# Moving weight preparation ahead of the image in a windowed-attention and convolution block

## The chip, the cores and the metric

The kernel runs on one core of one Trainium2 chip. A core has five engines that run side by side: TensorE (PE, matrix products), VectorE (DVE), ScalarE (ACT), GpSimd (POOL) and SyncE (SP), which here only issues transfers. Sixteen DMA engines move data between main memory (HBM) and the on-chip memory SBUF; matrix products land in a second on-chip memory, PSUM. Engines wait for each other and for transfers through semaphores. The metric is the device time of one launch in microseconds (us), as the median of several runs.

## The reference, cut to what matters

The input x is float32, 8 images of 384 channels and 64 x 64 pixels. Two layers follow each other:

```
x = x + attention(group_norm(x))          # layer 0
x = x + filtered_conv(group_norm(x))      # layer 1
```

`group_norm` takes 32 groups of 12 channels per image, and subtracts the mean and divides by the standard deviation over all pixels of a group. Layer 0 normalises each pixel over its 384 channels (`(xt - mu) / sqrt(var + eps) * norm_g + norm_b`), forms queries, keys and values by one product with `qkv_w`, and attends within 8 x 8 windows: half of the channels in plain windows, the other half in windows shifted by 4 pixels with a mask, four heads of 48 each with a table of position biases. A product with `proj_w` follows. Layer 1 is a product with `w_in`, a filter on the 8 x 8 Fourier transform of each block, a 3 x 3 convolution by channel, a gated gelu and a product with `w_out`.

## The kernel before, in words

**Tiling.** An image is cut into 8 strips of 8 rows (512 pixels, 8 windows). A strip in SBUF is 128 partitions by 3 chunks by 512 pixels, 0.79 MB. All products are in float32. A trace shows two matmul records for each matmul of the code.

**Schedule.** Every piece of work is a Python function, and a list `plan` holds pieces with a place on a time line (`at(place, piece, ...)`, L721 to L805). One unit of it is one window stage of attention; image b starts at 16 b. The list is sorted and the pieces are issued in that order (L811 to L827). Matmuls keep exactly this order on TensorE (`tc.keep_in_program_order` in `matmul`, L62). The other engines' instructions are placed by a scheduler unless they are held to the order in the same way. Ahead of the loop of L811, a count of TensorE instructions is kept for each piece (`FETCHES`, four for a matmul, two for a transpose); where `small_tiles` stands in the plan, up to 99 empty instructions are spread over neighbouring large matmuls so that the following dense run begins at a chosen position modulo 256 (`RUN_AT`).

**The prologue of the first image.** All loads of the start are issued at the top of the kernel. SP's queue takes the eight strips of the first image (`first_x`, L92), then the constants `cst` (identity, averaging matrices, masks; L95), the query and key weights in two raw tiles (`wqk_raw`, L113), the value weights `wv`, then `wp`, `w_in` (L119) and `w_out`. ScalarE's queue takes small vectors (`vec`, L141 and L143: gains and biases, most of them 4 bytes a row). GpSimd's queue takes the two tables of position biases in 64 transfers (`rpb_raw`, L171). A transfer increments one of eight semaphores that SP's and ScalarE's queues share, and it waits until the earlier transfer on its semaphore has landed.

Then, in the order of the plan: `input_stats` (L237) for the eight strips, `input_mean` and `input_std` (two tiny products, `pm_a` and `pv_a`), `group_normal` of the first strips (L328, gives y), and the sums for the normalisation over channels. That is three pieces. `ln_square` squares y on ScalarE (L333) and adds the three chunks on GpSimd (L335). `ln_sums` forms means of y (12 matmuls) and of the squares (4) with a matrix of ones, copies them, and computes the reciprocal standard deviation `rc` of 4 rows of 128 pixels. Those are written to DRAM as one line and read back to all 128 partitions (`rs`, L356 and L358). `ln_scale` multiplies y by `rs` (L363). The gain and the mean of that normalisation are worked into the weights instead: `pack_qk` copies the raw weights into 6 blocks per chunk (26 copies, L135), `qk_weights` (for each of the two branches) and `v_weights` form the bias from `lnb` (`pb`, `pv`), and `centre` scales by `lng` (L198), forms the column mean by three matmuls (`pc`) and subtracts it (L202).

In the plan, these stand at -3.02 (`pack_qk`), -2.9 (`qk_weights` of branch 0), -0.95 (`v_weights`) and -0.94 (`qk_weights` of branch 1), between the sums of the first strips.

**Attention.** The dense work begins with `qk_tile` (`pq`, L391), three tiles of three matmuls for a strip and a branch, evicted by ScalarE (L394), then `v_tile` (`pvv`), `scores` (`pS`), softmax, `turn` (`pT`), `apply` (`pA`), `put` and `project`. The second branch reads a shifted copy of two neighbouring strips, which GpSimd makes from the scaled y (L376 to L378).

Of the kernel before, what the change touches and what calls it, by code (L numbers as in the profile page):

```python
# [9 lines left out]
ALU = mybir.AluOpType  # L10
AX = mybir.AxisListType

P = 128
KC = 3
C = 384
# [3 lines left out]
NS = SW // WS  # L19
# [11 lines left out]
FETCHES = {"qk_tile": 12, "v_tile": 24, "project": 12, "scores": 128, "apply": 128, "turn": 16, "put": 16,  # L31
           "ln_sums": 64, "mix": 12, "transform": 32, "back": 192, "finish": 48, "input_mean": 4,
           "input_std": 4, "second_mean": 4, "second_std": 4, "filter_weights": 4, "out_bias": 36,
           "qk_weights": 48, "v_weights": 60}
RUN_AT = 208, 138


# [1 line left out]
def block_kernel(ctx: ExitStack, tc: tile.TileContext, out, x, consts, fsel, wqk, wv, bqk, bv,  # L39
                 wp, bp, lng, lnb, rpb1, rpb2, w_in, w_dw, w_out, filt):  # L40
    nc = tc.nc
# [8 lines left out]
    def psum(name):  # L50
        return ps.tile([P, ST], F32, tag="gemm", name=name)
# [9 lines left out]
    def matmul(*args, **kw):  # L61
        tc.keep_in_program_order(nc.tensor.matmul(*args, **kw))  # L62
        fetched["count"] += 4

        n = min(fetched["empty"], fetched["share"])
        for _ in range(n):
            tc.keep_in_program_order(nc.tensor.nop(hint="empty"))
        fetched["empty"] -= n
        fetched["count"] += n
# [5 lines left out]
    def strip(tag, bufs, name):  # L75
        return sb.tile([P, KC, ST], F32, tag=tag, bufs=bufs, name=name)
# [4 lines left out]

    def rows_of(img, s):

        return img[:, s * WS:(s + 1) * WS, :].rearrange("(p k) h w -> p k (h w)", k=KC)

    first_x = []
    for s in range(NS):
        tag, bufs = ("x", 5) if s < 5 else (("xn", 1), ("ow", 1), ("y2", 1))[s - 5]  # L90
        t = strip(tag, bufs, f"x_first{s}")
        nc.sync.dma_start(out=t, in_=rows_of(x[0], s))  # L92
        first_x.append(t)
    cst = cp.tile([P, N_CONST], F32, name="cst")
    nc.sync.dma_start(out=cst, in_=consts)  # L95
    ident = cst[:, C_ID:C_ID + P]
# [18 lines left out]
    wv_sb = cp.tile([P, KC, C], F32, name="wv_sb")  # L115
    wp_sb = cp.tile([P, KC, C], F32, name="wp_sb")
    wi_sb = cp.tile([P, KC, C], F32, name="wi_sb")
    for dst, src in ((wv_sb, wv), (wp_sb, wp), (wi_sb, w_in)):
        nc.sync.dma_start(out=dst, in_=src)  # L119
    wo_sb = cp.tile([P, 2, C], F32, name="wo_sb")  # L120
    nc.sync.dma_start(out=wo_sb[:, 0, :], in_=w_out[0:P])
# [6 lines left out]
        blocks += [(1, 96, 16, 1, 1, 32), (1, 112, 16, 1, 1, 96)] if j == 1 else [(j, 96, 32, 1, 1, c)]  # L128
    by_branch = wqk_sb.rearrange("p k (b j) c -> p k b j c", b=2)

    def pack_qk():
        for br in range(2):
            for i, (j, to, n, t, hp, of) in enumerate(blocks):
                eng = nc.gpsimd if br and i % 2 else nc.vector
                eng.tensor_copy(by_branch[:, :, br, j, to:to + n], raw_qk[t][:, :, br, hp, of:of + n])  # L135

    vec = cp.tile([P, 18], F32, name="vec")
    lng_sb, lnb_sb = vec[:, 0:3], vec[:, 3:6]
# [54 lines left out]

    bq_sb = cp.tile([P, 2, 6], F32, name="bq_sb")

    def centre(w):
        for k in range(KC):
            nc.vector.tensor_scalar(w[:, k], w[:, k], lng_sb[:, k:k + 1], None, ALU.mult)  # L198
        pc = psum("pc")
        for k in range(KC):  # L200
            matmul(pc[:, 0:C], ones_c, w[:, k], start=(k == 0), stop=(k == KC - 1))
        nc.vector.tensor_tensor(w, w, pc[:, 0:C].unsqueeze(1).to_broadcast([P, KC, C]), ALU.subtract)  # L202

    def qk_weights(br):
        pb = psum("pb")
        for j in range(3):
            for k in range(KC):
                matmul(pb[:, j:j + 1], wqk_sb[:, k, 3 * br + j, :], lnb_sb[:, k:k + 1],
                       start=(k == 0), stop=(k == KC - 1))
        own = bqk_sb[:, 3 * br:3 * br + 3]  # L210
        tc.keep_in_program_order(nc.vector.tensor_tensor(own, own, pb[:, 0:3], ALU.add))

        for i in range(2):
            nc.vector.tensor_scalar(bq_sb[:, i, 3 * br:3 * br + 3], own, pick[:, i:i + 1], None, ALU.mult)
        centre(wqk_sb[:, :, 3 * br:3 * br + 3].rearrange("p k j c -> p k (j c)"))

    def v_weights():
        pv = psum("pv")
        for lo, hi, kt, cols in ((0, P, 0, 0), (0, 64, 1, 192), (64, P, 1, 128), (0, P, 2, 256)):
            for k in range(KC):  # L220
                matmul(pv[lo:hi, kt:kt + 1], wv_sb[:, k, cols:cols + hi - lo], lnb_sb[:, k:k + 1],
                       start=(k == 0), stop=(k == KC - 1))
        nc.vector.tensor_tensor(bv_sb, bv_sb, pv[:, 0:3], ALU.add)
        centre(wv_sb)

    def out_bias():
        pp = psum("pp")
# [49 lines left out]
    def at(place, piece, *args):  # L277
        plan.append((place, len(plan), piece, args))
# [44 lines left out]
    def group_normal(b, s):  # L323
# [3 lines left out]
        for k in range(KC):  # L327
            nc.vector.tensor_scalar(by_window(y[:, k, :]), image_order(t[:, k, :]), gs[:, 0:1], gs[:, 1:2],  # L328
                                    ALU.subtract, ALU.mult)

    def ln_square(b, s):
        sq = ys[b, s, "sq"] = strip("sq", 1, f"sq_{b}_{s}")
        nc.scalar.activation(sq, ys[b, s], AF.Square)  # L333
        for k in (1, 2):
            nc.gpsimd.tensor_tensor(sq[:, 0, :], sq[:, 0, :], sq[:, k, :], ALU.add)  # L335

    def ln_sums(b, s):


        p = psum(f"ln_{b}_{s}")  # L340
        for to, t, n in ((0, ys[b, s], KC), (P, ys.pop((b, s, "sq")), 1)):
            for k in range(n):
                for j in range(4):
                    matmul(p[32 * j:32 * (j + 1), to:to + P], ones_c[:, 0:32], t[:, k, j * P:(j + 1) * P],
                           start=(k == 0), stop=(k == n - 1))
        m = sb.tile([P, 2 * P], F32, tag="lc", bufs=1, name=f"m_{b}_{s}")
        nc.scalar.copy(m, p[:, 0:2 * P])  # L347
        rc = sb.tile([P, P], F32, tag="lr", bufs=2, name=f"lr_{b}_{s}")
        nc.vector.tensor_tensor(rc, m[:, 0:P], m[:, 0:P], ALU.mult)  # L349
        nc.vector.tensor_tensor(rc, m[:, P:2 * P], rc, ALU.subtract)  # L350
        nc.scalar.activation(rc, rc, AF.Sqrt, bias=eps_t)
        nc.vector.reciprocal(rc, rc)

        line = dr.tile([4, P], F32, tag="line", bufs=4, name=f"line_{b}_{s}")
        queue = nc.scalar if b == 0 and s < 2 else nc.sync
        queue.dma_start(out=line, in_=rc[0:P:32, :])  # L356
        rs = ys[b, s, "rs"] = row512("rs", 2, f"rs_{b}_{s}")
        queue.dma_start(out=rs, in_=bass.AP(line.tensor, line.offset, [[0, P], [1, ST]]))  # L358

    def ln_scale(b, s):  # L360

# [359 lines left out]
    for b in range(B):  # L721
# [4 lines left out]
            at(u, load, b, s, "stats")  # L726
            at(u + (0.5 if b else 0.05), input_stats, b, s)
        if b == 0:
            at(-3.02, pack_qk)
            at(-2.9, qk_weights, 0)  # L730
            at(-0.95, v_weights)
            at(-0.94, qk_weights, 1)
            at(-0.9, position_bias, 0)
            at(-0.5, position_bias, 1)
            at(0.2, out_bias)
            at(0.2, filter_weights)
# [76 lines left out]
    for i, (piece, args) in enumerate(order):  # L813
        count += 4 * sum(on_pe[args[1]].values()) if piece is conv_taps else FETCHES.get(piece.__name__, 0)
        if piece in (qk_tile, project):
            dense.append(i)
        elif piece is scores:
            dense = []
        elif piece is small_tiles:
            n = (RUN_AT[args[0] % 2] - count - round(WAITS[0] * args[0] + WAITS[1])) % 256  # L820
            if n < 100:
                count += n
                for j in range(n):
                    empty[dense[j % len(dense)]] += 1
# [111 lines left out]
```

## Time and profile before

| | us |
|---|---|
| median of 3 runs | 3713.88 |
| lowest, highest | 3712.17, 3715.45 |
| the profiled execution's own time | 3717.37 |
| its span, from first to last instruction | 3715.4 |
| mean granted TensorE clock, share of full | 0.995 |

A line of the timeline gives the start in us from the first instruction, the duration, the engine, the line of the kernel, the operation, the tile written and the tiles read, shapes, and how many instructions were merged (x8). In brackets stands the idle time of that engine before it and who ended it; "issue" means that the profile shows no one. PEld is the loading of weights into TensorE. A row of the list of waits has the waiting engine and tile, the one waited for, the total in us, the number of waits and the longest. PEclk is the share of the full TensorE clock that was granted in a stretch.

### The profile page before, as it was taken

The numbers are of one execution on the slowest core, as the hardware profiler recorded it, in microseconds if no ns is written. First come the engines' busy times: TensorE is split into PE (matmuls) and PEld (weight loads), VectorE is DVE, ScalarE is ACT, GpSimd is POOL, SyncE is SP. The second block draws the span as 40 slices with busy tenths as digits, with TensorE's granted clock in tenths as the row PEclk, the third lists the DMA queues.
The fourth block names the chain that finished last, engine by engine and source line by source line (L and its number), as shares of the span: only waits on it lengthen the run. The fifth ranks groups of instructions, "written<-read, shape, count | busy, mean of one in ns | idle before, by whom it ended". The sixth has DMA issues, their size and how long they took to land.

```text
span 3715.4 us, 92922 instructions
## 1 busy us (share of the span) xinstructions
PE 3609.1 (97%) x38528; PEld 2340.4 (63%) x38528; DVE 2844.0 (77%) x4601; ACT 2383.0 (64%) x3946; POOL 435.1 (12%) x776
## 2 busy tenths in 40 slices
PE   4999999999999999999999999999999999999898
PEld 2666666666666666666666666666666666666554
DVE  4555568777887788787887778877788777777898
ACT  1766676666676576675776667676676766676442
POOL 5111111011111011101111011111011111110000
PEclk9999999999999999999999999999999999999999
DMA  4222222233232233222332332323232322222422
GB/s 122 80 89 75 92 100 102 87 111 109 101 123 84 89 134 109 104 94 104 107 130 84 109 106 101 132 82 105 88 131 102 107 89 84 100 81 81 154 103 77
DMA packets 144507, 377.34 MB, mean 102 GB/s; under 512 B 12308, under 2 KB 12900, under 8 KB 144100
## 3 DMA queue, kind: packets, MB, share of 16 engines
q1 hardware_dynamic: 139952, 370.60, 28.4%
q8 instruction: 319, 5.23, 0.6%
q0 software_dynamic: 2048, 0.15, 0.1%
q10 hardware_dynamic: 2100, 0.63, 0.1%
q14 instruction: 88, 0.72, 0.1%
HBM read 270.54 MB, written 100.79 MB: 100 GB/s over the span
## 4 chain that ended last, share of the span: by engine, by line
PE 86%; DVE 6%; DMA 4%; ACT 2%; issue 1%; POOL 0%; SPq 0%; DVEq 0%; ACTq 0%; POOLq 0%
PE pq L62 24%; PE pr L62 13%; PE pvv L62 12%; PE pt L62 12%; PE pw L62 6%; DVE zz L673 3%; PE pS L62 3%; PE pA L62 3%; PE pT L72 3%; PE po L72 3%; PE pz L62 3%; PE pf L62 2%; PE ln L62 2%; DMA x_norm<-in_x_dram 1%; DMA rpb_raw<-in_rpb_dram 1%
## 5 line engine op out<-in xcount | busy, mean ns | idle before, releaser
L673 DVE SCALAR_TENSOR_TENSOR zz<-z,dw_sb,zz 128x512 f32<-128x512 f32 x1490 | 1081.8, 751 | 23.7 <-ACT z L632 11.2
L62 PE MATMUL pq<-y,wqk_sb 128*128 128x512 f32 x2160 | 990.2, 596 | 0.0
L62 PEld LDWEIGHTS pq<-y,wqk_sb 128*128 128x128 f32 x2160 | 402.7, 190 | 437.1 <-issue 403.9
L62 PE MATMUL pt<-wi_sb,xn 128*128 128x384 f32 x1536 | 534.6, 486 | 0.0
L62 PE MATMUL pr<-oT,wp_sb 128*128 128x512 f32 x1152 | 523.1, 592 | 0.4 <-DVE oT L537 0.4
L62 PE MATMUL pvv<-wv_sb,y 128*128 128x192 f32 x2880 | 495.8, 326 | 0.0
L62 PEld LDWEIGHTS pvv<-wv_sb,y 128*128 128x128 f32 x2880 | 471.7, 190 | 36.2 <-issue 22.0
L394 ACT ACTIVATE qab<-pq,bq_sb,cst 96x512 f32<-96x512 f32 (+1 forms) x256 | 197.8, 772 | 401.9 <-PE pq L62 385.0
L62 PEld LDWEIGHTS pt<-wi_sb,xn 128*128 128x128 f32 x1536 | 286.1, 190 | 200.9 <-issue 44.0
L394 ACT ACTIVATE kcd<-pq,vec 32x512 f32<-32x512 f32 x512 | 348.4, 680 | 9.0
L62 PEld LDWEIGHTS pr<-oT,wp_sb 128*128 128x128 f32 x1152 | 211.1, 190 | 223.8 <-issue 212.3
L376 POOL COPY y<-y 128x384 f32<-128x384 f32 x112 | 100.0, 893 | 1529.4 <-PE pvv L62 1035.9
L335 POOL TENSOR_TENSOR sq<-sq 128x512 f32<-128x512 f32 x128 | 164.3, 1283 | 638.2 <-ACT sq L333 633.3
L584 ACT COPY t<-pt 128x384 f32<-128x384 f32 x256 | 124.1, 485 | 177.7 <-PE pt L62 174.5
L667 ACT ACTIVATE zz<-z,dw_sb 128x512 f32<-128x512 f32 x183 | 134.0, 733 | 159.0 <-PE pw L62 144.5
L349 DVE TENSOR_TENSOR lr<-m 128x128 f32<-128x128 f32 x64 | 19.7, 308 | 278.3 <-ACT m L347 278.3
L394 ACT ACTIVATE qcd<-pq,bq_sb,cst 96x512 f32<-96x512 f32 (+1 forms) x256 | 197.1, 770 | 44.4 <-PE pq L62 40.9
L428 ACT COPY v<-pvv 128x384 f32<-128x384 f32 x256 | 120.7, 477 | 160.2 <-PE pvv L62 159.2
L546 DVE SCALAR_TENSOR_TENSOR x_add<-pr,vec,x_add 128x512 f32<-128x512 f32 x192 | 143.4, 747 | 94.3 <-PE pr L62 92.6
L62 PE MATMUL pw<-zz,wo_sb 128*128 128x512 f32 (+1 forms) x512 | 182.4, 499 | 0.0
L394 ACT ACTIVATE kab<-pq,vec 96x512 f32<-96x512 f32 (+1 forms) x256 | 174.2, 680 | 9.0 <-PE pq L62 7.4
L72 PEld LDWEIGHTS pT<-cst,e 128*128 128x128 f32 x1024 | 119.1, 141 | 67.2 <-issue 39.8
(140 smaller groups left out, 5297.2 us busy)
## 6 DMA issues: line engine op xcount, KB each, us to landing
x_add<-in_x_dram SPq DMA_DIRECT2D x64, 768.0 KB
x1d<-x_add SPq DMA_DIRECT2D x64, 768.0 KB
x_mix<-x1d SPq DMA_DIRECT2D x64, 768.0 KB
x_finish<-x1d SPq DMA_DIRECT2D x64, 768.0 KB
out_dram<-x_finish SPq DMA_DIRECT2D x64, 768.0 KB
x_norm<-in_x_dram SPq DMA_DIRECT2D x61, 768.0 KB
x_stats<-in_x_dram SPq DMA_DIRECT2D x56, 768.0 KB
rs<-line SPq DMA_DIRECT2D x62, 256.0 KB
```

The costliest lines, as they stand in the source:

```text
L62: tc.keep_in_program_order(nc.tensor.matmul(*args, **kw))
L72: tc.keep_in_program_order(nc.tensor.transpose(*args, **kw))
L335: nc.gpsimd.tensor_tensor(sq[:, 0, :], sq[:, 0, :], sq[:, k, :], ALU.add)
L349: nc.vector.tensor_tensor(rc, m[:, 0:P], m[:, 0:P], ALU.mult)
L376: nc.gpsimd.tensor_copy(dst[:, :, :, :, 0:4], src[:, :, :, :, 4:8])
L394: return nc.scalar.activation(dst[to:to + n], pq[of:of + n], AF.Identity, bias=bias[of:of + n], scale=scale)
L428: nc.scalar.copy(v[:, 2 * g:2 * g + 2, :, 0:HD], pvv[:, 0:384].rearrange("p (g h d) -> p g h d", g=2, h=4))
L546: nc.vector.scalar_tensor_tensor(t[:, m, :], pr, bp_sb[:, m:m + 1], t[:, m, :], ALU.add, ALU.add)
L584: nc.scalar.copy(t1, pt[:, 0:C])
L667: nc.scalar.activation(zz.rearrange("p (r c) -> p r c", c=SW), z[:, 1:9, 1:SW + 1], AF.Copy, scale=dw_sb[:, m, 4:5])
L673: i = nc.vector.scalar_tensor_tensor(acc.rearrange("p (r c) -> p r c", c=SW), z[:, dy:dy + 8, dx:dx + SW], dw_sb[:, m, TAPS[tap]:TAPS[tap] ...
```

## The change

Four things are changed.

1. On SP's queue, `cst`, the two `wqk_raw` tiles and `wv` are issued ahead of the eight strips; `wp`, `w_in` and `w_out` stay behind them.
2. `pack_qk` and the weight pieces move in the plan between the statistics of the strips (places -9.97 to -9.44; strip s has its statistics at -9.95 + 0.1 s). All packing copies are on VectorE, and VectorE's part is held to the order of the plan. The subtraction of `centre` becomes a piece of its own, `take_off`, two strips later than the rest.
3. For the first three strips of the first image, GpSimd does not add the chunks of squares. `ln_sums` sums all three chunks on TensorE (12 matmuls instead of 4).
4. For the first strip, `rc` does not go through DRAM. `spread_first` multiplies it by columns of the identity, so that four matmuls write each row to all partitions of a PSUM tile, and `ln_scale` reads that tile.

The counts of `FETCHES` are adapted: 16 for `spread_first`, and 32 more for the sums of the first three strips.

```diff
-           "qk_weights": 48, "v_weights": 60}
+           "qk_weights": 48, "spread_first": 16, "v_weights": 60}
...
-    first_x = []
-    for s in range(NS):
-        tag, bufs = ("x", 5) if s < 5 else (("xn", 1), ("ow", 1), ("y2", 1))[s - 5]
-        t = strip(tag, bufs, f"x_first{s}")
-        nc.sync.dma_start(out=t, in_=rows_of(x[0], s))
-        first_x.append(t)
     cst = cp.tile([P, N_CONST], F32, name="cst")
     nc.sync.dma_start(out=cst, in_=consts)
...
-    for dst, src in ((wv_sb, wv), (wp_sb, wp), (wi_sb, w_in)):
+    nc.sync.dma_start(out=wv_sb, in_=wv)
+    first_x = []
+    for s in range(NS):
+        tag, bufs = ("x", 5) if s < 5 else (("xn", 1), ("ow", 1), ("y2", 1))[s - 5]
+        t = strip(tag, bufs, f"x_first{s}")
+        nc.sync.dma_start(out=t, in_=rows_of(x[0], s))
+        first_x.append(t)
+    for dst, src in ((wp_sb, wp), (wi_sb, w_in)):
         nc.sync.dma_start(out=dst, in_=src)
...
+    in_order = tc.keep_in_program_order
+
     def pack_qk():
         for br in range(2):
-            for i, (j, to, n, t, hp, of) in enumerate(blocks):
-                eng = nc.gpsimd if br and i % 2 else nc.vector
-                eng.tensor_copy(by_branch[:, :, br, j, to:to + n], raw_qk[t][:, :, br, hp, of:of + n])
+            for j, to, n, t, hp, of in blocks:
+                in_order(nc.vector.tensor_copy(by_branch[:, :, br, j, to:to + n],
+                                               raw_qk[t][:, :, br, hp, of:of + n]))
...
-    def centre(w):
+    means = {}
+
+    def centre(w, *key):
         for k in range(KC):
-            nc.vector.tensor_scalar(w[:, k], w[:, k], lng_sb[:, k:k + 1], None, ALU.mult)
+            in_order(nc.vector.tensor_scalar(w[:, k], w[:, k], lng_sb[:, k:k + 1], None, ALU.mult))
         pc = psum("pc")
         for k in range(KC):
             matmul(pc[:, 0:C], ones_c, w[:, k], start=(k == 0), stop=(k == KC - 1))
-        nc.vector.tensor_tensor(w, w, pc[:, 0:C].unsqueeze(1).to_broadcast([P, KC, C]), ALU.subtract)
+        means[key] = w, pc
+
+    def take_off(*key):
+        w, pc = means.pop(key)
+        in_order(nc.vector.tensor_tensor(w, w, pc[:, 0:C].unsqueeze(1).to_broadcast([P, KC, C]), ALU.subtract))
...
+    def summed(b, s):
+
+        return b > 0 or s > 2
+
     def ln_square(b, s):
         sq = ys[b, s, "sq"] = strip("sq", 1, f"sq_{b}_{s}")
         nc.scalar.activation(sq, ys[b, s], AF.Square)
-        for k in (1, 2):
+
+        for k in (1, 2) if summed(b, s) else ():
             nc.gpsimd.tensor_tensor(sq[:, 0, :], sq[:, 0, :], sq[:, k, :], ALU.add)
...
-        for to, t, n in ((0, ys[b, s], KC), (P, ys.pop((b, s, "sq")), 1)):
+        for to, t, n in ((0, ys[b, s], KC), (P, ys.pop((b, s, "sq")), 1 if summed(b, s) else KC)):
...
+        if (b, s) == (0, 0):
+            ys[b, s, "rc"] = rc
+            return
...
+    def spread_first():
+
+        rs, rc = psum("rs_first"), ys.pop((0, 0, "rc"))
+        for j in range(4):
+            matmul(rs[:, j * P:(j + 1) * P], ident[:, 32 * j:32 * j + 1].to_broadcast([P, P]), rc,
+                   start=True, stop=True)
+        ys[0, 0, "rs"] = rs
...
-            at(-3.02, pack_qk)
-            at(-2.9, qk_weights, 0)
-            at(-0.95, v_weights)
-            at(-0.94, qk_weights, 1)
+
+            at(-9.97, pack_qk)
+            at(-9.96, qk_weights, 0)
+            at(-9.84, take_off, "qk", 0)
+            at(-9.76, v_weights)
+            at(-9.64, take_off, "v")
+            at(-9.56, qk_weights, 1)
+            at(-9.44, take_off, "qk", 1)
+            at(-2.7, spread_first)
...
+        elif piece is ln_sums and not summed(*args):
+            count += 32
```

## The prediction

> **What bounds the kernel now.** I read the page's shares first, then the list of waits, then the timeline of the first 110 us, and last the granted clock in short stretches. Busy shares:
>
> ```profile
> PE 3609.1 (97%) x38528; PEld 2340.4 (63%) x38528; DVE 2844.0 (77%) x4601; ACT 2383.0 (64%) x3946; POOL 435.1 (12%) x776
> ```
>
> TensorE works 97% of the span. So only an interval in which it stands still, or work taken from it, can move the end. Its waits (total us, times, longest):
>
> ```profile
> PE pm_a L62 <- DVE mv_a L244: 31.7, 1, 31.7
> PE ln L62 <- POOL sq L335: 14.8, 1, 14.8
> PE pz L62 <- DVE t L601: 10.8, 15, 3.2
> ```
>
> The two longest occur once each, before any attention work, and they are what the change addresses. The timeline (start, us, engine, what) shows what stands before the first dense matmul:
>
> ```profile
> 28.92 1.88 DVE L237 BATCH_NORM_STATS2 st<-x_first 128x6 f32<-128x512 f32 x3 [0.55 <-DMA x_first<-in_x_dram]
> 30.84 0.80 DVE L244 BATCH_NORM_AGGREGATE mv_a<-st 128x2 f32<-128x144 f32 x1
> 34.23 1.68 DVE L328 TENSOR_SCALAR y<-x_first,gs_a 128x512 f32<-128x512 f32 x3
> 35.94 1.48 ACT L333 ACTIVATE sq<-y 128x1536 f32<-128x1536 f32 x1 [1.94 <-DVE y L328]
> 38.88 9.02 POOL L171 DMA_DIRECT2D rpb_raw<-in_rpb_dram x15 [1.56 <-DMA rpb_raw<-in_rpb_dram]
> 48.44 1.40 POOL L335 TENSOR_TENSOR sq<-sq 128x512 f32<-128x512 f32 x1
> 51.47 0.65 PE L62 MATMUL ln<-sq,cst 128*32 128x128 f32 x8 [14.85 <-POOL sq L335]
> 52.05 4.00 PE L62 MATMUL pb<-vec,wqk_sb 128*128 128x1 f32 x18
> 55.91 4.33 PE L62 MATMUL pc<-wqk_sb,cst 128*128 128x384 f32 x6
> 71.49 0.35 ACTq L358 DMA_DIRECT2D rs<-line  x1
> 74.94 1.75 DVE L363 TENSOR_TENSOR y<-y,rs 128x1536 f32<-128x1536 f32 x1
> 78.22 8.10 PE L62 MATMUL pq<-y,wqk_sb 128*128 128x512 f32 x18
> 110.55 0.34 PE L62 MATMUL pS<-kcd,qcd 64*64 64x64 f32 x8 [0.68 <-issue]
> ```
>
> The statistics follow the strips as they land and end at 30.8. The first squares are ready at 37.4, but their summing on GpSimd stands in program order behind 64 small table loads, which it issues until 47.9. After that come the weights: two of pb and three of pc plus pv, from 52 to 78, with TensorE at half clock for most of it. The first dense matmul, pq, starts at 78.22, and from there TensorE hardly stops. So the price of the prologue is 78.2 us, and the change is worth what it takes off that number, less what it adds later.
>
> The clock (stretch, us, PE, PEld, DVE, ACT, POOL, PEclk, DMA share, GB/s):
>
> ```profile
> 28.00:30.00 2.00, 0.00 (x0) 0.00 (x0) 1.45 (x3) 0.00 (x0) 2.00 (x5) 1.00 1.07 379
> 70.00:72.00 2.00, 2.00 (x11) 2.00 (x11) 1.34 (x1) 0.00 (x0) 1.12 (x4) 0.50 0.00 1
> ```
>
> [...] clock 0.50 from 65.0 to 78.6, pq matmuls 640 ns apart before 78.9 and 430 after. [...] the DMA share is about 1 from 4 to 36 us, whatever queue feeds it. [...] scaling strip 0 from PSUM should cost the 1.75 us of L363. No run here shows that yet.
>
> **The change, part by part**, as a new prologue.
>
> *1. Loads.* Constants (0.49 MB), wqk (1.57) and wv (0.59) go ahead of the eight strips (6.29 MB) on SP. Summed over stretches like those above, 7.5 MB were moved until 28.9, a good 1 MB of it beyond the last strip. With 2.65 MB more ahead and 1 MB of later loads alongside as now, 1.4 to 2.6 MB remain at that point; at the 320 to 380 GB/s of 22 to 30 us the last strip lands 3 to 8 us later: 32 to 37. The built order also shows that a load waits for an earlier one's semaphore: strip 0 for a small bias load that itself waits for wqk, strip 2 for strip 0, strip 7 for strip 1. A small load under this traffic took 3.6 us (issued 12.1, its successor released 16.1). I estimate strip 0 at 15, strip 1 at 18, strips 2 and 3 at 20 and 22.5. SP's later loads (wp, w_in, w_out) are needed only past 70.
>
> *2. Preparation between statistics.* VectorE now does, in this order: 26 packing copies; bias, scaling of q and k; strips 0 and 1; the subtraction; the same for v; strips 2 and 3; and so on. The second half of wqk lands at about 9.6 (2.07 MB from 2.3 us at 280 GB/s). Half the copies at 0.135 us (nine in 1.22) end at 11, and pb of branch 0 (18 matmuls at 213 ns, half clock, 3.9) at 14.2. The bias add waits for all small bias loads too, the last of which waits for wv (11.7): 15.8. Then, with pc 3.85 (six at 640 ns) and pv 3.3 (2.1 at full clock) on TensorE:
> - bias and scaling 0.5 + 1.2: 17.5; two strips 3.8: 21.3; subtraction 1.35: 22.7.
> - pc from 16.8 to 20.65, pv to 24.0. v bias and scaling 1.3: 25.3; two strips: 29.1; subtraction: 30.4.
> - pc of v 24.65 to 28.5, pb of branch 1 to 32.4. Bias and scaling 1.7: 34.1; two strips: 37.9; subtraction: 39.2; last two strips: 43.0.
>
> So the statistics end at 43 instead of 30.8, bounded by VectorE and half-clock TensorE and not by the loads. If TensorE is granted full clock in part of it, up to 3.4 less; if the small loads are 3 us later, 3 more.
>
> *3. From mean to first pq.* Aggregate to first normal took 3.4 (30.84 to 34.23): 46.4; normal 1.68: 48.1; square 1.48: 49.6. The POOL sum is gone; TensorE sums three chunks, 24 matmuls instead of 8. Eight took 0.58 at half clock; 1.7: 51.3. Copy 0.37, two vector operations 0.6; the square of strip 1 stands ahead of the root on ScalarE: root ends 53.65, reciprocal 0.95: 54.65. spread_first: eight matmuls of 128 columns, at 213 ns 1.7: 56.4, in place of the two DMAs, which took from 58.9 to 67.2. Scaling 1.75: 58.3. TensorE does strip 1's sums meanwhile (2.7), to about 59.2: **first pq at 59.2, 19.0 earlier.**
>
> *4. What is given back.* pq now starts at half clock; 1 to 3 us until it is released cost half of that: 1.5. In before only 0.2 was lost so. Strip 2's sums stand in dense work with 16 matmuls more: 0.7 (eight took 0.33 start to start). Strip 1's row still goes by DRAM, and its two DMAs now stand on ScalarE between evictions: the first behind one of pq's first tile, the second behind one of the second tile. From the issue 71.49 to the scaling 74.94 are 3.45; with 7.2 after the first pq for the second issue, scaling and three GpSimd copies end at 13.6 after it. The matmul that reads them is due at 13.0 (91.24 less 78.22) plus 1.5: 0.3 taken for a stall, bounds 0 and 3.
>
> *5. Instruction positions.* 96 + 16 instructions more ahead of the second image lead the planner to leave out 112 empty ones. These cost nothing: six pq with empties take 2.84 as six without. Counted on the built order, windows from the third of the second image on move by 2 in 256; the 17 before by about 112. Among those 17, two dense runs have a hole (0.68 and 0.91). The new positions could make 0 to 4 such holes: 0, bounds -1.6 and +2.
>
> Sum: -19.0 + 1.3 + 0.7 + 0.3 = -16.7; taken as **-16**. The profiled execution took 3717.4, with a span of 3715.4; its successor's span would be 3699.4. The three runs have their median at 3713.9, 3.5 below that execution, so the forecast is **3698**.
>
> **The rivals.**
> - *A, as worked out* (0.62): 3694 to 3703.
> - *B, full clock comes early in the preparation and small loads land early* (0.17): statistics end near 37, pq at 53.5: -22, 3692. For it: pc and pv together are 7 us without a long gap. Against: before, pb and pc ran 9.5 us until the clock rose at 61.6.
> - *C, the row of strip 1 is late* (0.12): ScalarE waits inside its evictions, TensorE loses 3 to 7 us more: 3703. For it: the order of issues. Against: the 1 us of room.
> - *D, the change does little* (0.06): strips chained by semaphores arrive one by one, 4 us each; statistics end at 54, pq at 70: 3709.
> - *E, slower* (0.03): [...] Each window meets a hole of 0.9 where it had none; it decides only from 27 of 128 windows on (16 + 7.4 over 0.9), as 3722. Against: positions move by 2 in all but 20 of them.
>
> **How the numbers follow.** A measurement of this kernel can tell about 0.2%, 7.4 us, from no change. A, B and C lie beyond it on the fast side: 0.91. D is 0.06 within it, E 0.03 slower. The likeliest is A's 3698. A and B reach down to 3690, C up to 3706; outside are D, E and tails of B and C.
>
> **What would show it.** In the profile after: no wait of TensorE on POOL's sq in the first image; the last BATCH_NORM_STATS2 at 41 to 45, with VectorE idle less than 3 us since 16 and then for PE pv and pb; spread matmuls of 1 to 1.8 us; the first pq at 56 to 62, at a clock of 0.5 for under 4 us; no new wait over 1 us in the first window; and everything past it shifted whole. I am wrong if the statistics wait for x_first strips again, if pq's second tile or the shifted strip's pq waits for ScalarE or POOL for over 2 us, or if later windows differ in length.

## The result, and the profile after

The changed kernel takes 3693.96 us (median of 4 runs, 3690.8 to 3696.07), beside 3713.03 us (4 runs, 3711.4 to 3715.45) for the kernel before: a ratio of 0.995, 95% interval 0.9938 to 0.9961, or 19.1 us less. Forecast were 16 us less. A second set of 5 runs, taken with the later experiments, gave 3695.86 us, ratio 0.9949 (0.9937 to 0.9961).

The shares of the page are nearly what they were, TensorE at 98% (97% before):

```profile
PE 3610.3 (98%) x38584; PEld 2342.0 (63%) x38584; DVE 2841.1 (77%) x4607; ACT 2384.6 (65%) x3946; POOL 426.9 (12%) x764
```

TensorE's waits (total us, times, longest). Of the two long ones of before, the 14.8 for `sq` from POOL is gone and the 31.7 for `mv_a` is down to 6.0. The longest ones that stand in the prologue now:

```profile
PE pb L62 <- DMA vec<-in_bqk_dram: 11.0, 1, 11.0
PE pc L62 <- DVE wqk_sb L204: 6.1, 2, 5.0
PE pm_a L62 <- DVE mv_a L254: 6.0, 1, 6.0
PE rs_first L62 <- DVE lr L367: 3.2, 1, 3.2
```

The timeline of the changed kernel (its line numbers are some 10 to 26 higher than before: statistics L247, scaling of a strip L389):

```profile
7.83 0.48 DVE L138 COPY wqk_sb<-wqk_raw 128x144 f32<-128x144 f32 x3 [6.96 <-DMA wqk_raw<-in_wqk_dram]
10.98 4.00 PE L62 MATMUL pb<-vec,wqk_sb 128*128 128x1 f32 x18 [10.98 <-DMA vec<-in_bqk_dram]
19.03 0.16 DVE L221 TENSOR_TENSOR vec<-vec,pb 128x3 f32<-128x3 f32 x1 [5.46 <-DMA dw_sb<-in_w_dw_dram]
23.96 2.32 PE L62 MATMUL pv<-vec,wv_sb 128*128 128x1 f32 x24
40.05 3.64 DVE L247 BATCH_NORM_STATS2 st<-x_first 128x6 f32<-128x512 f32 x6
50.28 1.51 PE L62 MATMUL ln<-sq,cst 128*32 128x128 f32 x24 [0.83 <-ACT sq L347]
55.03 2.04 PE L62 MATMUL rs_first<-lr,cst 128*128 128x128 f32 x8 [3.24 <-DVE lr L367]
57.11 1.75 DVE L389 TENSOR_TENSOR y<-y,rs_first 128x1536 f32<-128x1536 f32 x1 [2.23 <-PE rs_first L62]
59.21 7.99 PE L62 MATMUL pq<-y,wqk_sb 128*128 128x512 f32 x18
72.12 2.84 PE L62 MATMUL pq<-y,wqk_sb 128*128 128x512 f32 x6
89.21 1.15 PE L62 MATMUL pA<-v,eT 64*64 64x49 f32 x64
```

The weights are packed from 7.8 and done before the image's statistics end at 43.7 (they ended at 30.8 before). From there a chain of latencies leads to the first pq at 59.21 instead of 78.22: 19.0 earlier. The first apply (`pA`) stands at 89.21 instead of 107.89: 18.7 earlier, so nearly all of the gain is kept through the first windows. At the second apply it is 19.6, since the hole of 0.68 that the kernel before had right behind its first apply is not there, and it stays within 0.1 of that for the rest of the first image: what follows is shifted whole. The clock, in the columns of the table before:

```profile
56.00:58.00 2.00, 2.00 (x26) 1.71 (x28) 0.89 (x1) 0.00 (x0) 0.00 (x0) 0.50 0.00 0
60.00:62.00 2.00, 2.00 (x6) 0.87 (x5) 1.14 (x3) 1.46 (x2) 1.16 (x4) 1.00 0.00 0
```

TensorE is at half clock until 58.6 and at full clock when pq starts; the spreading and the sums of strip 1 run on it from 55.0 on, just ahead of pq. In all eight profiled executions that have the two right ahead of pq (the changed kernel twice, and six of the versions below), full clock comes between 0.6 us before and 0.7 us after the start of pq; in the version without the spreading, where TensorE stands still for 8.85 us ahead of pq, it comes 5.0 after.

The two profiled executions differ by 23.7 us of span (3715.4 and 3691.7), more than the medians. The execution profiled for before, 3717.37, lay above the four runs of this comparison, so 19.1 is the number to explain. The traces have 18.7 of it by the first apply and 19.6 by the second.

### The profile page after: what moved, and what is told of

Its sections match the earlier page's. It is cut to its first block, busy times and chain, and to the rows that moved or that the text cites. A ratio compares the mean times of both kernels' runs of the same rounds, so it can differ in the third digit from the quotient of the medians.

```text
span 3691.7 us, 92911 instructions
## 1 busy us (share of the span) xinstructions
PE 3610.3 (98%) x38584; PEld 2342.0 (63%) x38584; DVE 2841.1 (77%) x4607; ACT 2384.6 (65%) x3946; POOL 426.9 (12%) x764
## 4 chain that ended last, share of the span: by engine, by line
PE 87%; DVE 6%; DMA 3%; ACT 2%; issue 1%; SPq 0%; ACTq 0%; DVEq 0%
PE pq L62 25%; PE pr L62 13%; PE pvv L62 12%; PE pt L62 12%; PE pw L62 6%; DVE zz L699 3%; PE pS L62 3%; PE pA L62 3%; PE po L72 3%; PE pT L72 3%; PE pz L62 3%; PE pf L62 2%; PE ln L62 2%; DMA x_norm<-in_x_dram 1%; DMA x1d<-x_add 0%
## 5 line engine op out<-in xcount | busy, mean ns | idle before, releaser
L699 DVE SCALAR_TENSOR_TENSOR zz<-z,dw_sb,zz 128x512 f32<-128x512 f32 x1490 | 1082.0, 751 | 23.7 <-ACT z L658 11.2
L364 DVE TENSOR_TENSOR lr<-m 128x128 f32<-128x128 f32 x64 | 18.7, 292 | 281.0 <-ACT m L362 281.0
L350 POOL TENSOR_TENSOR sq<-sq 128x512 f32<-128x512 f32 x122 | 156.6, 1284 | 628.1 <-ACT sq L347 623.3
```

The lines of the kernel that those rows point to most:

```text
L699: i = nc.vector.scalar_tensor_tensor(acc.rearrange("p (r c) -> p r c", c=SW), z[:, dy:dy + 8, dx:dx + SW], dw_sb[:, m, TAPS[tap]:TAPS[tap] ...
```

## The experiments

Each adds parts of the change to the kernel before, leaves one out of the changed kernel, or builds on the changed kernel. "Statistics" is the end of the last one of the first image, "pq" the start of the first dense matmul, both in the profiled execution. Each ratio is taken against runs of the kernel before that were made together with that experiment (their medians: 3712.9 to 3713.6).

| kernel | time us (range, runs) | ratio to before, 95% | statistics | pq |
|---|---|---|---|---|
| before | 3713.0 | 1 | 30.8 | 78.2 |
| changed | 3693.96 (3690.8 to 3696.1, 4) | 0.9938 to 0.9961 | 43.7 | 59.2 |
| before + part 3 | 3697.82 (3695.0 to 3700.5, 4) | 0.9942 to 0.9972 | 30.9 | 59.4 |
| before + part 1 | 3715.61 (3713.3 to 3719.1, 12) | 0.9999 to 1.0016 | 39.8 | 79.5 |
| before + parts 3, 4 | 3697.31 (3696.9 to 3702.0, 4) | 0.9945 to 0.9972 | 30.7 | 60.6 |
| changed, no part 3 | 3697.22 (3696.3 to 3701.4, 5) | 0.9945 to 0.9974 | 42.8 | 60.7 |
| changed, no part 4 | 3705.69 (3702.2 to 3708.9, 13) | 0.9970 to 0.9986 | 43.6 | 63.9 |
| changed, no part 1 | 3714.03 (3710.6 to 3715.5, 12) | 0.9992 to 1.0009 | 65.4 | 81.1 |

### The squares alone

The kernel before with part 3 only:

```diff
-        for k in (1, 2):
+        for k in (1, 2) if summed(b, s) else ():
             nc.gpsimd.tensor_tensor(sq[:, 0, :], sq[:, 0, :], sq[:, k, :], ALU.add)
```

> The kernel before, with only the squares of the first three strips summed on TensorE. Theory (the two long waits before the first pq are one chain: GpSimd's queue, then 26 us of weight preparation on TensorE): the first sums are ready near 38.5 instead of 52.1, the 26 us follow, the first pq moves from 78.2 to 65 (63 to 68), the time falls by 10 to 14, to about 3701. Rival (the preparation waits for something else that ends near 60 to 70, the GpSimd copies of branch 1 or the row by DRAM): pq at 74 or later, less than 5 us gained.

Measured: 3697.82 us, and the first pq at 59.40, earlier than expected. The timeline of this kernel:

```profile
37.34 1.51 PE L62 MATMUL ln<-sq,cst 128*32 128x128 f32 x24 [0.86 <-ACT sq L337]
51.24 2.17 PE L62 MATMUL pc<-wv_sb,cst 128*128 128x384 f32 x6 [1.00 <-DVE wv_sb L198]
51.67 1.75 DVE L367 TENSOR_TENSOR y<-y,rs 128x1536 f32<-128x1536 f32 x1
59.40 8.23 PE L62 MATMUL pq<-y,wqk_sb 128*128 128x512 f32 x18
89.63 1.15 PE L62 MATMUL pA<-v,eT 64*64 64x49 f32 x64
```

The sums of the squares come at 37.34 instead of 51.47, 14.1 earlier, and the weights follow at once. From the sums to the first pq it takes 22.1 us instead of 26.8, because the products from 46.6 to 55.3 ran at the speed of full clock (24 matmuls of ln in 0.86, which take 1.51 at half clock; pc of v in 2.17; pb of the second branch in 2.06, which took 3.84 at a clock of 0.50 in the kernel before). So this one part, with the weights where they were, brings the first pq to the place where the whole change brings it, and 15 of the 19 us. At the first apply its trace is only 0.4 behind the changed kernel's (89.63 and 89.21). The rest of the 2 to 4 us between the medians was not traced to a cause, and the two intervals overlap: what the other three parts add to this one is small and not settled.

### The change without the squares

> The changed kernel with the first squares summed on GpSimd again. Theory (GpSimd's table loads end near 46.4, before the squares are ready at 50.2, so that its queue holds nothing back any more): only 2.7 us of GpSimd work less 0.9 of TensorE work come onto the path, first pq at 61 to 63, time 2 to 4 us above the changed kernel. Rival (GpSimd's queue is still what counts): first pq later by 10 us or more.

```diff
     def summed(b, s):
-        return b > 0 or s > 2
+        return True
```

Measured: 3697.22 us, pq 1.5 later, though the statistics end 0.9 earlier: from the squares to pq it takes 11.3 us instead of 9.0. That the same part is worth 15 us in one kernel and 1.4 to 3.3 in the other is explained by this timeline, of the changed kernel without part 3:

```profile
41.52 7.46 POOL L175 DMA_DIRECT2D rpb_raw<-in_rpb_dram  x13
50.13 2.75 POOL L350 TENSOR_TENSOR sq<-sq 128x512 f32<-128x512 f32 x2
52.93 0.66 PE L62 MATMUL ln<-sq,cst 128*32 128x128 f32 x8 [4.35 <-POOL sq L350]
```

GpSimd has issued its table loads by 49.0, and the squares are ready on ScalarE only at 49.4, because the statistics end 12 us later. There is no queue of table loads left for the sum to stand in; only some clearing of tiles puts its start off to 50.1. It costs its own 2.75 us and this wait, less what the larger sums on TensorE took.

### The loads alone, and the change without them

The kernel before with part 1 only:

```diff
-    for dst, src in ((wv_sb, wv), (wp_sb, wp), (wi_sb, w_in)):
+    nc.sync.dma_start(out=wv_sb, in_=wv)
+    first_x = []
...
+    for dst, src in ((wp_sb, wp), (wi_sb, w_in)):
```

> The kernel before, with only the order of the loads changed (constants, wqk, wv ahead of the strips). Theory: the last statistics end 3 to 8 us later (near 36), which is hidden, because the squares still wait for GpSimd's queue until about 48 to 51; first pq between 77 and 80, time within 2 us of before. Rival (the loads decide): the whole chain moves by the 5 us that the strips are late, to about 3719.

It gives 3715.61 us: 2.6 more than before, and the interval reaches 1. Statistics end 9 us later than before, and it does not matter, since the sums of the squares on GpSimd still wait for its table loads. The line of the timeline to compare with 51.47 before:

```profile
52.82 0.66 PE L62 MATMUL ln<-sq,cst 128*32 128x128 f32 x8 [7.40 <-POOL sq L336]
```

The opposite, the changed kernel with the strips again ahead of the weights on SP's queue:

```diff
+    first_x = []
+    for s in range(NS):
...
     cst = cp.tile([P, N_CONST], F32, name="cst")
     nc.sync.dma_start(out=cst, in_=consts)
```

> The changed kernel with only the order of the loads undone: the strips come first, the plan stays. Theory (the preparation stands in VectorE's order ahead of the statistics, so the weights' arrival starts the whole chain): packing starts at 30 to 34 instead of 8 to 11, first pq near 78 (74 to 84), the gain is gone, 3707 to 3719. Rival (VectorE's order matters little, the strips' arrival does): first pq below 65.

Measured: 3714.03 us. All of the gain is gone, as expected. VectorE works in its written order, so the statistics wait for weights that land last: the packing begins at 33.1, and the last statistics stand behind it at 61.7. Its timeline:

```profile
33.09 0.48 DVE L138 COPY wqk_sb<-wqk_raw 128x144 f32<-128x144 f32 x3 [32.22 <-DMA wqk_raw<-in_wqk_dram]
61.73 3.65 DVE L247 BATCH_NORM_STATS2 st<-x_first 128x6 f32<-128x512 f32 x6
```

So part 2 needs part 1: parts 2, 3 and 4 gain nothing here, though parts 3 and 4 alone gain 16 us (below). Part 1 alone gains nothing either, with GpSimd's queue still in place; parts 1 and 3 without part 2 were not run.

### The change without the spreading

> The changed kernel without spread_first: the first row goes by DRAM again. Theory (the row is on the path): the two transfers with their waits take 5.1 to 8.3 us where the four matmuls took 2.0, first pq at 62 to 66, time 3 to 6 us above the changed kernel, near 3698. Rival (strip 1's sums on TensorE hide it): first pq unchanged within 1 us.

```diff
-        if (b, s) == (0, 0):
-            ys[b, s, "rc"] = rc
-            return
...
-            at(-2.7, spread_first)
```

Measured: 3705.69 us, 11.7 above the changed kernel (9.8 above its second set) and two to three times what I had expected. It is also 8 us above the kernel with part 3 alone (3697.82), with no overlap of the ranges: moving the weights ahead, without the spreading, costs more than it brings. The first pq is 4.7 later, at 63.94. The first apply, at 98.08, stands 34.1 after it instead of 30.0, which makes 8.9 at that point. The timeline of this kernel:

```profile
58.86 1.41 ACTq L373 DMA_DIRECT2D rs<-line  x2
62.13 3.43 DVE L386 TENSOR_TENSOR y<-y,rs 128x1536 f32<-128x1536 f32 x2 [3.25 <-DMA rs<-line]
63.94 10.43 PE L62 MATMUL pq<-y,wqk_sb 128*128 128x512 f32 x18 [8.85 <-DVE y L386]
84.81 7.11 PE L62 MATMUL pq<-y,wqk_sb 128*128 128x512 f32 x12
```

and its granted clock in the stretch behind the first pq:

```profile
64.00:69.00 5.00, 5.00 (x6) 2.13 (x7) 4.67 (x9) 0.00 (x0) 4.83 (x9) 0.51 0.00 0
```

TensorE stands still for 8.85 us ahead of pq and then runs at half clock until 68.9. The first 18 matmuls take 10.43 instead of 7.99 us. The trace has it at half clock once more, with 0.50 from 86 to 89, and 12 matmuls take 7.11 instead of 5.42. These two differences, 2.44 and 1.69, are the whole 4.1. Only the first stands behind the wait. Ahead of the second TensorE had been busy since 63.94; the clock fell after a stretch that held the one-column products `pp` (82.0 to 84.0), and the same 12 matmuls are slow in the version with parts 3 and 4, where TensorE had not stood still for more than 0.9 us since 46.5:

```profile
80.08 6.67 PE L62 MATMUL pq<-y,wqk_sb 128*128 128x512 f32 x12
```

Whether the later start brought this second stretch about was not tested. The row of strip 1 has nothing to do with it: both rows landed together and both strips were scaled by 65.6. The rest, 1 to 3 us, lies in later stages and was not traced to a cause.

To see whether the clock can be had back, seven products nobody reads were put into TensorE's wait, ahead of pq:

```diff
+    def keep_busy():
+        p = psum("busy")
+        for k in range(7):
+            matmul(p[:, 0:C], ones_c, wv_sb[:, k % KC], start=(k == 0), stop=(k == 6))
...
+            at(-0.95, keep_busy)
```

> The changed kernel without part 4, plus seven 384-column products on TensorE whose result nobody reads, in the 8.8 us in which it waits for the row of strip 0 ahead of the first pq. Without part 4 the first pq came 4.7 us later, and the first apply another 4.1 us later after it (34.1 instead of 30.0). My theory: these 4.1 us are a TensorE at half clock after standing still (5 us until 68.9, and a window at 86). Kept busy, it starts pq at full clock: first pq at 63 to 65, first apply 30.0 to 31.7 after it, time 3700 to 3703, that is 3 to 5 below the kernel without part 4 (3705.7). Rival: the 4.1 us come from the two transfers of each row on ScalarE's queue among its evictions or from late y of the shifted strip; then the first apply stays 34 after the first pq and the time stays at 3705 to 3707.

Measured: 3702.51 us (8 runs, 3699.9 to 3706.5), 3.2 lower, but with ranges that overlap. The profiled execution, 3706.52, is the slowest of the eight and shows why this settles little:

```profile
55.40 4.78 PE L62 MATMUL busy<-wv_sb,cst 128*128 128x384 f32 x14
64.31 9.69 PE L62 MATMUL pq<-y,wqk_sb 128*128 128x512 f32 x18 [4.12 <-DVE y L391]
```

The 14 matmuls ran at full clock (0.34 us each; those of pc, as wide, took 0.36 at full clock and 0.64 at half) and were over in 4.78 us. TensorE then stood still for 4.12, and the clock fell inside pq, about 1 us from its start: the weight loads take 0.19 us up to 64.84, 0.33 from 65.37 on and 0.19 again from 68.68. The first apply came 33.4 after pq, and 0.75 of the 2.44 behind the wait was won back in this execution. The second stretch at half clock came again in spite of the filler, with loads of 0.33 from 86.00 to 88.56 and 7.11 for the 12 matmuls; my expectation had put both stretches down to the standing still. That the 4.1 are half-clock matmuls is shown by the lines above; that a longer filler would win back the 2.44 was not shown.

### The spreading without the weights

The kernel before with parts 3 and 4 asks whether the spreading is worth anything where the weights stand in the old place.

```diff
...
+        if (b, s) == (0, 0):
+            ys[b, s, "rc"] = rc
+            return
...
+            at(-2.7, spread_first)
```

> The kernel before with parts 3 and 4 alone (weights neither loaded nor prepared earlier). With part 3 alone TensorE stood still for at most 1.0 us at a time between 46.6 and the first pq at 59.4, since the products of v and of the second branch stand in its order there. My theory: part 4 shortens a chain that does not end last in this order, so it is worth nothing without parts 1 and 2; the eight spreading matmuls are added to TensorE (0.9 to 2.0 us), first pq at 59.5 to 61, time 3697 to 3700. Rival: the row's way through DRAM is on the path here too (scaling of strip 0 at 51.7, and it could be at 48.8), so the first pq comes 3 us earlier, at 56 to 57, and the time is 3693 to 3695.

Measured: 3697.31 us, first pq at 60.56, as my theory had it and not its rival:

```profile
48.46 1.75 DVE L378 TENSOR_TENSOR y<-y,rs_first 128x1536 f32<-128x1536 f32 x1 [0.35 <-PE rs_first L62]
60.56 8.69 PE L62 MATMUL pq<-y,wqk_sb 128*128 128x512 f32 x18
```

Strip 0 is scaled 3.2 earlier than with part 3 alone (48.46 instead of 51.67), and nothing follows from it: TensorE still has the weights of v and of the second branch ahead of pq; the last group of these starts at 57.63. By the medians the spreading is worth 0 here and 10 to 12 us in the changed kernel. (In this profiled execution the first apply is at 92.91, 3.3 later than with part 3 alone: 1.2 from the first pq, and most of the rest from matmuls that ran at half clock for a part: 8.69 us for the 18 and 6.67 for the 12, where full clock has 7.99 and 5.42.)

### What binds the preparation

Once the weights are there, VectorE's longest idle time in the changed kernel's prologue is the 5.46 us ahead of 19.03. There the bias add waits for small loads on ScalarE's queue (the profile names `dw_sb`, issued right behind the last bias load), and scaling, product and statistics stand behind it. This kernel moves the bias adds to just ahead of the subtraction:

```diff
     def take_off(*key):
         w, pc = means.pop(key)
+        bias[key]()
...
-        tc.keep_in_program_order(nc.vector.tensor_tensor(own, own, pb[:, 0:3], ALU.add))
+        def add():
+            in_order(nc.vector.tensor_tensor(own, own, pb[:, 0:3], ALU.add))
...
+        bias["qk", br] = add
```

> The changed kernel with each bias addition moved from before the scaling to just ahead of the subtraction. In the changed kernel VectorE stands 5.46 us from 13.6 to 19.0, until the last small bias load has landed. Theory (the statistics are bound by VectorE's chain, not by the strips): that wait is filled, the statistics end at 39 to 41 instead of 43.7, first pq at 55 to 57, time 3 to 5 us below the changed kernel, near 3690. Rival (strips or TensorE at half clock bind): less than 1.5 us gained.

Measured: 3693.01 us (3691.0 to 3695.2, 4 runs), statistics at 43.9, first pq at 59.6. The wait is gone, the end is where it was, and the time is 1 to 3 us lower with overlapping ranges, where 3 to 5 had been expected. The trace does not bear out the theory that this wait binds. The timeline:

```profile
22.74 1.88 DVE L251 BATCH_NORM_STATS2 st<-x_first 128x6 f32<-128x512 f32 x3 [3.50 <-DMA x_first<-in_x_dram]
26.25 1.07 DVE L204 TENSOR_SCALAR wv_sb<-wv_sb,vec 128x384 f32<-128x384 f32 x3
```

VectorE now waits 3.50 for strip 1 to land at 22.7. The scaling of v then starts at 26.25, where it was in the changed kernel (26.39). In this execution the 5.46 had been cover for a load. It does not settle the size: here the weights had landed 0.8 to 1.3 later than in the changed kernel, and in the next version, with the same late adds, strip 1 was there at 20.8. That pv took longer here (3.61 us instead of 2.32) did not count, since it ended at 23.7, ahead of strip 1's statistics.

My next theory was that what binds is that every step of the weights takes its turn in VectorE's order. With the late adds kept, the scaling of v and of the second branch on ScalarE, which is idle:

```diff
-            in_order(nc.vector.tensor_scalar(w[:, k], w[:, k], lng_sb[:, k:k + 1], None, ALU.mult))
+            if key == ("qk", 0):
+                in_order(nc.vector.tensor_scalar(w[:, k], w[:, k], lng_sb[:, k:k + 1], None, ALU.mult))
+            else:
+                in_order(nc.scalar.activation(w[:, k], w[:, k], AF.Copy, scale=lng_sb[:, k:k + 1]))
```

> late_bias, with the scaling of the v weights and of branch 1 on ScalarE, which is idle until 44. Theory (VectorE's work bounds): 2.2 us of VectorE work go and the products can start earlier, statistics end at 36 to 38.5, first pq 2 to 3 us before late_bias. Rival (the arrival of the last strips near 33 to 36, or the chain of products at half clock, has become the bound): no gain on late_bias.

Measured: 3691.04 us (3689.0 to 3692.3, 4 runs), ratio 0.9937 (0.992 to 0.9953):

```profile
20.87 1.63 ACT L207 ACTIVATE wv_sb<-wv_sb,vec 128x384 f32<-128x384 f32 x3 [18.19 <-PE pv L62]
54.09 7.99 PE L62 MATMUL pq<-y,wqk_sb 128*128 128x512 f32 x18
```

The scaling of v starts right behind pv at 20.87 instead of 26.39, the statistics end at 38.3, and the first pq is at 54.1, 5.1 earlier. So the steps on VectorE did hold the statistics back; how much of the 5.1 belongs to the late adds, and how much to the scaling, these two executions with their different landing times do not tell. Last, two of the subtractions were moved to just ahead of the first pq, out of the statistics' way:

```diff
+            at(-9.841, add_bias, "qk", 0)
...
-            at(-9.64, take_off, "v")
+            at(-9.64, add_bias, "v")
+            at(-0.88, take_off, "v")
...
-            at(-9.44, take_off, "qk", 1)
+            at(-9.44, add_bias, "qk", 1)
+            at(-0.87, take_off, "qk", 1)
```

> The version with late bias adds and with the scaling of v and of the second branch on ScalarE, and in addition the subtractions of v and of the second branch (1.35 us each on VectorE) moved from between the statistics to just ahead of the first pq. VectorE had no idle time from 24.3 to the end of the statistics at 38.3, so they should end 2.7 earlier, at 35.6, unless the last strip has not landed by then, and the first pq comes at 51.5 instead of 54.1. My theory, that the first pq sets the time: 3688 to 3690, 4 to 6 below the changed kernel. Rival: the loads or later stages take it up, first pq at 53 to 54 and 3691, or the shifted strip's pq waits (its subtraction or the row of strip 1 late) and it is 3692 to 3694.

For comparison the changed kernel was run again, with no edit:

> The changed kernel as it is, beside the version above on the same chip, so that the two can be compared: 3692 to 3696, first pq at 59 to 60.

Measured: 3690.54 us (3688.6 to 3692.8, 5 runs), beside 3695.86 (3692.2 to 3697.5, 5 runs) for the changed kernel on the same chip. Against the version before it nothing is won: the statistics end at 39.0 and the first pq comes at 54.95. As the rival had it, the loads took it up, which the last statistics show:

```profile
37.10 1.88 DVE L256 BATCH_NORM_STATS2 st<-x_first 128x6 f32<-128x512 f32 x3 [0.31 <-DMA x_first<-in_x_dram]
```

With 2.7 us taken off VectorE, it waits for strips down to the last one (in an execution whose weights landed 1.0 to 1.3 later than in the version before it). Both versions lie some 3 to 5 us under the changed kernel. Their intervals against before overlap with its interval, so the order is likely and not more.

### The positions

My rival on the slow side was E, holes in the dense runs that come with the positions of instructions, and the change hardly moves positions. This kernel moves every dense run by 128 instructions:

```diff
-RUN_AT = 208, 138
+RUN_AT = 80, 10
```

> The changed kernel with both chosen positions of dense runs moved by 128 (RUN_AT = 80, 10). A test of the mechanism behind rival E. [...] holes of 0.5 to 1.1 us in about 50 windows, 20 to 55 us slower than the changed kernel, with the prologue unchanged. If positions don't matter: within 3 us of the changed kernel.

Measured: 3734.46 us (3732.8 to 3735.7, 4 runs), ratio 1.0054 (1.0039 to 1.0069), 40 us above the changed kernel. In its list of waits, and in that of the changed kernel:

```profile
PE pS L62 <- issue: 31.7, 49, 1.1
```

```profile
PE pS L62 <- issue: 1.6, 4, 0.7
```

The kernel before had 2.7 in 5 times there. All dense runs of pA and pS together, each from its first matmul to the one behind it, last 294.2 us instead of 253.5 in the changed kernel. This difference of 40.7 is the whole loss, and 30 of it stand in the lists as waits. That position decides on them is shown, for this one shift. What makes them at these positions is not shown: the lists have "issue" there and nothing that was waited for.

## Why the prediction was right, and where it was not

**Step 1, loads.** Estimated were strips 0 and 1 at 15 and 18, and the last between 32 and 37. In the changed kernel no statistic waits for a strip, so it does not show it. The kernel with part 1 only has the same order of loads, and each of its statistics waits for its strip: the first begin at 18.7 and 21.8, the last here:

```profile
37.93 1.88 DVE L238 BATCH_NORM_STATS2 st<-x_first 128x6 f32<-128x512 f32 x3 [0.42 <-DMA x_first<-in_x_dram]
```

With late bias adds, strips 0 and 1 came at 17.1 to 18.0 and 20.8 to 22.7. I had them some 2 to 5 us too early, and the last one just beyond my bound. The sum did not rest on it: the changed kernel begins the last two strips' statistics only at 40.05.

**Step 2, preparation.** The second half of wqk came at 10.7 (9.6), pb ended at 15.0 (14.2), and the bias add came at 19.0 (15.8): the 3 us for late small loads that the text kept as a bound came in full. The statistics ended at 43.7 (43.0) all the same, since TensorE was granted its full clock from 24.5 to 27.9 (pv took 2.32 where 3.3 was taken, pc of v 3.22 where 3.85 was). Errors of opposite sign cancelled, and that is luck: the second execution of the changed kernel ended its statistics at 41.9. I read the wait for the small loads as part of the sum; in the one profiled execution with late adds, taking it away alone freed nothing.

**Step 3, from mean to first pq.** 16.2 us were taken from the end of the statistics, 15.5 were measured. The squares ended at 50.2 (49.6), spreading took 2.04 (1.7), scaling from PSUM 1.75 (1.75). First pq: 59.21, predicted 59.2, and 58.03 in the second execution.

**Step 4, what is given back.** This is the step that failed, by its size. Of 2.3 us, 0.4 was measured. The 1.3 for a pq that starts at half clock was 0: the clock rose at 58.6, ahead of pq at 59.21, and the 18 matmuls took 7.99. (That pq would wait 1 to 3 us for the rise was my estimate and no trace had shown it; it was also set high, since half of 1 to 3 us is 0.5 to 1.5, of which I took the upper end.) The 0.3 for strip 1's row was 0: the shifted strip's pq came at 72.12, 12.9 after the first (13.0 before). The 0.7 for strip 2's sums was 0.4: from them to the first apply it is 0.77 us instead of 0.34.

**Step 5, positions.** The two holes of before, 0.68 and 0.91, are gone, which is the lower bound that I gave (-1.6); but the second execution of the changed kernel has one of 0.67 at 473, so part of this is chance. Rival E was priced soundly, since it asked for 27 windows with a hole of 0.9 to turn the sign, and 49 holes of 0.65 on average came with a loss of some 40 us; and it was rightly thought unlikely.

So -19.0 + 0.4 = -18.6 for the prologue, against 18.7 in the trace and 19.1 in the medians. By mechanism it was rival A, and by time it lies between A and B: what I had kept back for the clock was not needed.

**A reading.** The prediction has pq matmuls 640 ns apart before 78.9. The ones 640 apart are those of pc; only one pq starts before the clock rises at 78.6, and its 640 span the rise. Nothing in the sum hangs on it.

**What I did not ask.** The prediction priced the four parts as one new prologue and never said what each is worth. It lists the GpSimd queue of 64 table loads as what holds the first sum, and still takes part 3 as one term among others. Part 3 alone gives 15 of the 19 us, because it undoes the wait at its place. Parts 1, 2 and 4 together give 16 without it, because they put other work into the wait. Together they give 19 and not 31, since both remove the same wait. The two moves of the weights are not safe by themselves: with part 3 in place, adding part 1 and part 2 without the spreading makes the kernel 8 us slower, and adding part 2 and the spreading without part 1 makes it some 16 us slower.

## What to carry to other kernels

Find the one wait that stands ahead of everything, here a sum on GpSimd behind transfers that it was issuing, and ask for the smallest change that undoes it before reordering what stands around it; two remedies for the same wait do not add up. The value of a part depends on the order around it (the spreading 0 or 10 to 12 us, the sums 1 to 3 or 15), so price it in the kernel in which it will run. A long idle time on an engine has no price until it is known what comes next behind it: here the landing of a strip stood right behind 5.46 us of it.

## What the hardware showed that I had not expected

- **When the granted clock rises and falls differs from execution to execution, and the products take other times with it.** The same preparation had full clock at 24.5 to 27.9 and 38.1 to 41.6 in one execution of the changed kernel and at 23.4 to 26.8, 30.3 to 33.7 and 37.1 to 40.5 in the other, which had its first pq at 58.0 instead of 59.2; pb of the second branch, 3.84 us at half clock in the first, took 2.50 there.
- **Standing still cost twice.** Without the spreading, 8.85 us of waiting for a row cost 4.7 us in the start of pq and 2.4 more in matmuls at half clock right behind it.
- **The clock fell behind products of one column, but not behind all of them.** In the kernel before it was full from 61.6 to 65.0, while 2.17 us of pv (one column) and 0.91 of pc ran, and was 0.50 from 65.0 to 78.6. In the version without the spreading it fell near 86, some 2 us behind `pp` (one column, 2.06 us). In the changed kernel the same `pp` ran from 74.80 to 76.86, and the clock stayed full. What such products count for the clock was not shown. In the first 15 us the clock column shows 1.00, though pb took 4.00 there (2.06 at full clock in the kernel with part 3 only); up to the first recorded change (24.5 there, 61.6 in the kernel before) it tells nothing of the rate.
- **Positions of instructions.** A shift by 128 alone, with the same work, costs some 40 us, 1.1% of the kernel, in holes of up to 1.1 us inside dense runs of small matmuls.
